# A perceiver block: two norms in a row as one, a bank for each chunk of the late tokens' input product, B and C of the first pair by products with rows of ones

## The chip, the core and the metric

The kernel runs on one core of a Trainium2 chip. The time is the device time of one execution in microseconds (us). Five engines work side by side: TensorE (PE in the profile; its weight loads are PEld), VectorE (DVE), ScalarE (ACT), GpSimd (POOL) and SyncE (SP), which here only issues DMAs. Each engine runs its own instructions in order and waits on semaphores for the others. Products of TensorE land in PSUM, which has 8 banks of 512 fp32 values per partition.

## The reference, cut to what matters

The input is x of 8 batches by 64 tokens by 512, so 512 tokens in all. Three blocks follow each other, each added to x.

```
x = x + cross_attention(layernorm(x), ctx)                 # 16 heads, 1601 context rows, masked
x = x + two_track_mamba(layernorm(x))                      # its own first step is a layernorm too
x = x + mixture_of_experts(layernorm(x))                   # 8 experts, 2 for each token

def layernorm(x):      m = mean(x); v = var(x); return (x - m) / sqrt(v + 1e-5)
def mamba(h):          # h: the normed tokens; d_inner 1024, n 16, r 64; two tracks with other weights
    x, z  = split(h @ in_w.T)
    x     = silu(causal depthwise conv of width 4 (x) + conv_b)
    x_dbl = x @ x_w.T                                      # 64 columns for dt, 16 for B, 16 for C
    dt    = softplus(x_dbl[:, :64] @ dtp_w.T + dtp_b)
    per step: h = exp(dt * A) * h + (dt * x) * B ;  y = sum over n of h * C
    return ((y + x * D) * silu(z)) @ mout_w.T
```

Two layernorms without weights stand between the first addition and the products of mamba: that of the block and mamba's own, whose weight and bias (`nw`, `nb`) are applied after it.

## The kernel before, in words

The context that the mask lets through is at most 400 rows here, and the kernel has a path for that case, which is the one that runs (`narrow`). A second path for the general case is in the program as well and does not run.

**Attention.** A loop over 8 batches, in each of which 4 pairs of heads are done while the next batch's K and V are projected. Every second batch a group of 128 tokens is complete, and `out_product(c)` multiplies it with the output weights (tile `ap`, L424), adds it to x (L425), and norms it twice (`layernorm_chunk`, lines L86 to L97: statistics on DVE, Ln and Exp on ACT for the reciprocal root, one Newton step on DVE, and the subtraction and scaling of 128x512). `normed(c, l1)` transposes the result on TensorE (`tpl`, L435) and writes it, with weight and bias, to `oT` (L437). The first three groups are done inside the loop. The fourth comes after it: its tokens are called the late tokens (`LATE = T - P`).

**Start of mamba.** For the first track the product with `in_w` and the convolution are done early for the first 384 tokens (`x_early`, beside the last batch). For the late 128 tokens they follow the last `normed`: `in_product` (L237) makes 8 chunks of 128 channels, four to a PSUM tile of one bank (`ipl`), so two tiles. `begin(c)` on ACT (L732) scales a chunk by the conv's last weight, `convolved` on DVE adds the other three weights (L257, three instructions for a chunk), ACT applies Silu to the whole chunk of 512 tokens (L742), and TensorE multiplies it with `x_w` into `xd` (`x_product`, L276). In `begin` and `convolved` the order is written out by hand with `keep`, which holds an instruction to the order of the program on its engine. Where it isn't used a scheduler chooses.

**From xd to the first scan.** ACT copies `xd` to `xdb` (96 rows: 64 for dt, 16 for B, 16 for C; L281). SP writes the B and C rows to HBM (`bcd`, L283) and reads them back, each row broadcast to all partitions, in 8 loads of 1 MB, one for each pair of state numbers n (`load_bc`, L793, tile `bc`). Meanwhile `dt_product` (L801), `dt_act`, `dt_log` and `dt_rest` make dt and du = dt * x of the first chunk. Then the loop over 8 chunks times 8 pairs runs: ACT makes `da` in PSUM (exp, L1032), POOL makes `db` = du * B (L1036), DVE scans (`hs`, L996) and multiplies by C (`hc`, L1005), TensorE sums the pairs up (`yp`, L1015). Column 0 of each batch in `da` is set to zero once (L784). Jobs that `beside` lists are done between the pairs: the other track's input product (`ix`), its convolution, the next chunk's dt.

**PSUM pools.** In the first part: `mm` 3 banks, `tp` 2, `sp` 2, `op` 1. In the second: `da0` and `da1` 2 each, `hs` 2, `mm` 1, `yp` 1.

Of the kernel before, what the change touches and what calls it, by code (L numbers as in the profile page):

```python
# [10 lines left out]
F32 = mybir.dt.float32  # L11
# [6 lines left out]
P = 128  # L18
B, S, D = 8, 64, 512
T = B * S  # L20
# [29 lines left out]
def perceiver_block(ctx: ExitStack, tc: tile.TileContext, a: dict, out: bass.AP):  # L50
# [11 lines left out]
    make_identity(nc, ident)  # L62
    eps = const.tile([P, 1], F32, name="eps")
    nc.gpsimd.memset(eps, EPS)
    one = const.tile([P, 1], F32, name="one")
    nc.gpsimd.memset(one, 1.0)
    mean_f = const.tile([P, P], F32, name="mean_f")
# [2 lines left out]
    def col(name, i, n=1):  # L70
        o = _COLS[name][0] + i
        return vec[:, o : o + n]
# [6 lines left out]
        nc.vector.reciprocal(rs, std)  # L79
        return rs  # L80

    def layernorm_chunk(dst, src):

        st = small.tile([P, 6], F32, tag="lcst", name="lcst")
        mv = small.tile([P, 2], F32, tag="lcmv", name="lcmv")
        nc.vector.bn_stats(st, src)  # L86
        nc.vector.bn_aggr(mv, st)
        rs = small.tile([P, 1], F32, tag="lcrs", name="lcrs")
        nc.scalar.activation(rs, mv[:, 1:2], AF.Ln, bias=eps)
        nc.scalar.activation(rs, rs, AF.Exp, scale=-0.5)  # L90
        var = small.tile([P, 1], F32, tag="lcva", name="lcva")
        nc.vector.tensor_scalar(var, mv[:, 1:2], eps, -0.5, ALU.add, ALU.mult)
        r2 = small.tile([P, 1], F32, tag="lcr2", name="lcr2")
        nc.vector.tensor_tensor(r2, rs, rs, ALU.mult)
        nc.vector.tensor_scalar(r2, r2, var, 1.5, ALU.mult, ALU.add)
        nc.vector.tensor_tensor(rs, rs, r2, ALU.mult)
        nc.vector.tensor_scalar(dst, src, mv[:, 0:1], rs, ALU.subtract, ALU.mult)  # L97
# [97 lines left out]
    def block(general):  # L195
# [4 lines left out]
        with ExitStack() as ctx:  # L200
# [34 lines left out]
            def in_product(ip, iw, u, o=0, n=T):  # L235
                for k in range(ND):
                    nc.tensor.matmul(  # L237
                        ip, iw[:, k, u * P : (u + 1) * P], oT[k][:, o : o + n], start=(k == 0), stop=(k == ND - 1)
                    )
# [47 lines left out]
            with tc.tile_pool(name="at1", bufs=1) as at1, tc.tile_pool(name="at2", bufs=2) as at2, tc.tile_pool(  # L287
# [129 lines left out]
                def out_product(c):  # L417

                    tok = slice(c * P, (c + 1) * P)
                    for k in range(ND):  # L420
                        nc.scalar.activation(oT[k][:, tok], oT[k][:, tok], AF.Identity, bias=col("bv", k))
                    ap_ = pa.tile([P, D], F32, tag="mm", bufs=3, name="ap")
                    for k in range(ND):
                        nc.tensor.matmul(ap_, oT[k][:, tok], wo[:, k, :], start=(k == 0), stop=(k == ND - 1))  # L424
                    nc.vector.tensor_tensor(xr[:, c, :], xr[:, c, :], ap_, ALU.add)  # L425
                    l1 = vtile("l1")
                    layernorm_chunk(l1, xr[:, c, :])
                    layernorm_chunk(l1, l1)
                    return l1

                def normed(c, l1):
# [288 lines left out]


                xd = pa.tile([P, 2, 512], F32, tag="sp", bufs=1, name="xd0")[:, 0, :]
                ips = []
                for q in range(2):
                    ip = pa.tile([P, 4, P], F32, tag="mm", bufs=3, name="ipl")
                    for i in range(4):
                        in_product(ip[:, i, :], iws[q * 2 + i // 2], i % 2, LATE, P)
                        ips.append(ip[:, i, :])

                def begin(c):  # L730
                    w = c * DCONV + DCONV - 1
                    keep(nc.scalar.activation(  # L732
                        xs[0][c][:, LATE:], ips[c], AF.Identity, scale=col("cw0", w), bias=col("cb0", c)
                    ))

                for c in range(2):
                    begin(c)
                for c in range(NCH):
                    convolved(0, c, ips[c], LATE, P, begun=True)
                    if c + 2 < NCH:  # L740
                        begin(c + 2)
                    keep(nc.scalar.activation(xs[0][c], xs[0][c], AF.Silu))  # L742
                    x_product(xd, 0, c)
                x_done(0, xd)
# [20 lines left out]
            with tc.tile_pool(name="mb1", bufs=1) as mb1, tc.tile_pool(name="mb2", bufs=2) as mb2, tc.tile_pool(  # L765
# [14 lines left out]
                def by_batch(v):  # L780
                    return v.rearrange("p (b s) -> p b s", s=S)

                for da in das:
                    nc.vector.memset(da.rearrange("p n (b s) -> p (n b) s", s=S)[:, :, 0:1], 0.0)  # L784

                def bank(name):
                    return pm.tile([P, T], F32, tag="mm", name=name)

                def load_bc(t, n):

                    bcd, tiles = bcs[t]
                    tiles[n] = mb1.tile([P, 2, 2, T], F32, tag="bc", bufs=NS // 2 + 1, name=f"bc{t}_{n}")
                    nc.sync.dma_start(  # L793
                        tiles[n].rearrange("p o n t -> p o (n t)"),
                        bcd[:, n : n + 2, :].rearrange("o n t -> o (n t)").partition_broadcast(P),
                    )
# [36 lines left out]

                for n in range(0, NS, 2):
                    load_bc(0, n)
                e, r = dt_act(0, 0, dt_product(0, 0))
                for step in dt_rest(nc.vector, 0, 0, e, r, dt_log(e)):
                    pass
                ahead = {(0, 0): step}

                comb_all = mb1.tile([P, ND, T], F32, name="comb")
                comb = [comb_all[:, m, :] for m in range(ND)]
# [712 lines left out]
```

## Time and profile before

| what | value |
|---|---|
| median of 3 runs | 1346.03 us (1344.24 to 1346.55) |
| the profiled execution's own time | 1351.73 us |
| its span, first to last instruction | 1350.1 us |
| mean granted TensorE clock | 0.972 |
| busy: PE, DVE, ACT, POOL | 1197.1, 827.0, 572.4, 512.5 us |
| last group's `ap` added to x (L425) starts | 381.03 us |
| first late product (L237) starts | 388.91 us |
| `xdb` copy (L281) starts | 408.95 us |
| first scan (L996) starts | 421.72 us |

How to read it: all times within an execution are counted from the span's start. In answers of the trace a row has start, length, engine, line, operation, output and inputs, how many were merged, and in square brackets how long the engine was idle before it and what ended that. The chain of waits is followed back from the last instruction: at each step it names what released it. The windows give the busy time of each engine in a stretch of time, the granted clock of TensorE as a share of its full clock, the share of the DMA engines that were busy, and GB/s. Line numbers are those of the kernel before.

### The profile page before, as it was taken

Reading aid. Unit: us, or ns where it says so; the run is one execution under the profiler, and the core shown is the slowest. Engines: PE = TensorE matmul, PEld = TensorE weight load, DVE = VectorE, ACT = ScalarE, POOL = GpSimd, SP = SyncE. Lnnn points to the kernel's source line nnn. Section 1 sums busy time; section 2 is a strip of 40 time slices with the busy share of each in tenths; the row PEclk is TensorE's granted clock in tenths of the full one; section 3 lists DMA queues with packets and bytes.
Section 4 is the critical chain, followed back from the end, with each engine's and each line's share of the span. In section 5 each row is a group of like instructions: output and inputs, shape, how many; then the busy total and the mean of one; then the engine's idle time right before and its main releaser. Section 6 shows DMA issues by size and latency. Waiting matters only on the chain.

```text
span 1350.1 us, 14093 instructions
## 1 busy us (share of the span) xinstructions
PE 1197.1 (89%) x5030; PEld 718.1 (53%) x5030; DVE 827.0 (61%) x1226; ACT 572.4 (42%) x1152; POOL 512.5 (38%) x384
## 2 busy tenths in 40 slices
PE   4999999999976889889889988879799999999992
PEld 2444454444542333333333333324699999999981
DVE  5144443545756999999999999994423433443332
ACT  1133333333234566665655555550134523453440
POOL 4200000000024788888888888850210221022130
PEclk9999999999978999999999999999699999999996
DMA  6329900000027000100701010110891673476432
GB/s 226 132 67 300 298 3 1 0 1 0 1 79 262 16 31 1 31 16 23 267 17 31 16 47 17 54 31 2 318 348 61 238 285 120 167 285 260 167 118 68
DMA packets 95051, 148.71 MB, mean 110 GB/s; under 512 B 5968, under 2 KB 63584, under 8 KB 90864
## 3 DMA queue, kind: packets, MB, share of 16 engines
q1 hardware_dynamic: 89856, 131.31, 29.0%
q0 software_dynamic: 5104, 16.30, 3.4%
q8 instruction: 44, 0.72, 0.2%
q14 instruction: 47, 0.39, 0.1%
HBM read 122.95 MB, written 24.64 MB: 109 GB/s over the span
## 4 chain that ended last, share of the span: by engine, by line
PE 59%; DVE 28%; ACT 7%; DMA 2%; issue 2%; another core or an unknown queue 0%; POOL 0%; DVEq 0%; SPq 0%; POOLq 0%; ACTq 0%
DVE hs L996 17%; PE yp L1406 10%; PE hp L1361 9%; PE kp L393 7%; PE vp L551 6%; DVE hc L1005 6%; ACT da L1032 4%; PE yp L1015 3%; PE op L603 3%; PE sp L565 2%; PE atp L590 2%; PE ipe L237 2%; PE atp L591 2%; PE ap L424 1%; PE ip L852 1%
## 5 line engine op out<-in xcount | busy, mean ns | idle before, releaser
L1036 POOL TENSOR_TENSOR db<-du,bc 128x1024 f32<-128x1024 f32 x128 | 301.7, 2358 | 103.3 <-DVE hs L996 81.8
L996 DVE TENSOR_TENSOR_SCAN hs<-da,db 128x1024 f32<-128x1024 f32 x128 | 293.9, 2296 | 20.3 <-POOL db L1036 5.6
L1015 PE MATMUL yp<-hc,ident 128*128 128x512 f32 x512 | 248.1, 608 | 57.8 <-DVE hc L1005 57.0
L1032 ACT ACTIVATE da<-dt,an 128x504 f32<-128x504 f32 x256 | 174.9, 683 | 172.0 <-DVE hs L996 166.1
L1015 PEld LDWEIGHTS yp<-hc,ident 128*128 128x128 f32 x512 | 91.9, 190 | 202.6 <-DVE hc L1005 118.7
L1005 DVE TENSOR_TENSOR hc<-hs,bc 128x1024 f32<-128x1024 f32 x128 | 156.7, 1224 | 11.2 <-DVE hs L996 0.9
L1361 PE MATMUL hp<-xgT,w 128*128 128x192 f32 (+1 forms) x1024 | 155.0, 311 | 3.5 <-DVE xgT L1333 3.0
L1406 PE MATMUL yp<-h,w 128*128 128x192 f32 (+1 forms) x1024 | 151.8, 310 | 4.4 <-ACT h L1391 4.4
L1361 PEld LDWEIGHTS hp<-xgT,w 128*128 128x128 f32 x1024 | 150.5, 193 | 5.3 <-DVE xgT L1333 3.7
L1406 PEld LDWEIGHTS yp<-h,w 128*128 128x128 f32 x1024 | 149.2, 193 | 5.3 <-ACT h L1391 4.8
L393 PE MATMUL kp<-ctx,wk 128*128 128x400 f32 x256 | 93.6, 511 | 0.0
L383 POOL COPY qbd<-qT 32x256 f32<-32x256 f32 x32 | 12.6, 394 | 208.9 <-PE sp L565 207.6
L551 PE MATMUL vp<-wv,ctx 128*128 128x512 f32 x192 | 88.2, 604 | 0.0
L1368 ACT ACTIVATE h<-hp,ev 128x192 f32<-128x192 f32 (+1 forms) x128 | 50.8, 398 | 82.2 <-PE hp L1361 82.0
L1324 POOL DMA_DIRECT2D xg<-x_rows x11 | 6.0, 544 | 185.5 <-PE xtp L1330 175.8
L614 DVE COPY oT<-op 32x64 f32<-32x64 f32 x64 | 13.7, 215 | 93.6 <-PE op L603 93.2
L393 PEld LDWEIGHTS kp<-ctx,wk 128*128 128x128 f32 x256 | 46.4, 190 | 44.1 <-issue 14.1
L1423 DVE BATCH_NORM_STATS2 bs<-ytp 128x6 f32<-128x512 f32 (+1 forms) x13 | 8.5, 688 | 98.2 <-PE ytp L1421 98.2
L852 PE MATMUL ip<-oT,iw 128*128 128x512 f32 x128 | 60.6, 597 | 4.4 <-ACT x L910 3.3
L571 DVE CUSTOM_DVE_ANT_0 sc<-sp,madd,rsc 128x400 f32<-128x400 f32 x64 | 38.1, 629 | 38.7 <-PE sp L565 38.6
L1391 ACT ACTIVATE h<-h,ev 128x192 f32<-128x192 f32 (+1 forms) x128 | 55.9, 518 | 5.5 <-DVE h L1388 5.2
L1343 DVE TENSOR_TENSOR s<-h 128x768 f32<-128x768 f32 (+1 forms) x16 | 13.7, 857 | 72.1 <-ACT h L1368 72.1
(282 smaller groups left out, 1590.2 us busy)
## 6 DMA issues: line engine op xcount, KB each, us to landing
w<-in_w_dram SPq DMA_DIRECT2D x64, 1024.0 KB, 14.9
bc<-bcd SPq DMA_DIRECT2D x16, 1024.0 KB, 9.9
x_rows<-z SPq DMA_DIRECT2D x8, 1152.0 KB, 12.2
y_rows<-z SPq DMA_DIRECT2D x8, 1152.0 KB, 12.1
ctx<-in_ctx_dram SPq DMA_DIRECT2D x32, 200.0 KB, 4.0
iw<-in_fast_in_w_dram SPq DMA_DIRECT2D x8, 512.0 KB, 3.9
iw<-in_slow_in_w_dram SPq DMA_DIRECT2D x8, 512.0 KB, 3.5
mo<-in_slow_mout_w_dram SPq DMA_DIRECT2D x8, 512.0 KB, 4.0
```

The costliest lines, as they stand in the source:

```text
L393: nc.tensor.matmul(kp[:, :n], wk[:, k, ec * P : (ec + 1) * P], ctx_t[k][:, o : o + n], start=(k == 0), stop=(k == ND - 1),)
L551: nc.tensor.matmul(vp, ctxs[b][k][:, j * P : (j + 1) * P], wv[:, k, :], start=(k == 0), stop=(k == ND - 1))
L852: keep(nc.tensor.matmul(s[key], w[:, k, u * P : (u + 1) * P], oT[k], start=(k == 0), stop=(k == ND - 1)))
L996: keep(nc.vector.tensor_tensor_scan(hs.rearrange("p n s -> p (n s)"), q["da"].rearrange("p n s -> p (n s)"), q["db"].rearrange("p n s -> p ...
L1005: keep(nc.vector.tensor_tensor(q["hc"], hs, bcs[t][1][n][:, 1], ALU.mult))
L1015: keep(nc.tensor.matmul(yp[0], ident, q["hc"][:, j, :], start=False, stop=(n + j == NS - 1)))
L1032: keep(nc.scalar.activation(by_batch(da[:, j, :])[:, :, 1:], by_batch(dt)[:, :, 1:], AF.Exp, scale=an[:, t, k : k + 1]))
L1036: keep(nc.gpsimd.tensor_tensor(db, du.rearrange("p (o s) -> p o s", o=1).to_broadcast([P, 2, T]), bc[:, 0], ALU.mult))
L1361: nc.tensor.matmul(hp, st["w1"][k][:, i * P : (i + 1) * P], st["xgT"][:, k, :n], start=(k == 0), stop=(k == ND - 1),)
L1368: nc.scalar.activation(h[:, i, :], hp, AF.Relu, bias=st["ev"][:, i : i + 1])
L1391: nc.scalar.activation(h[:, i, :], h[:, i, :], AF.Identity, bias=st["ev"][:, NF + f : NF + f + 1], scale=st["ev"][:, f : f + 1],)
L1406: nc.tensor.matmul(yp, ws[i // 4][:, i % 4, m * P : (m + 1) * P], st["h"][:, i, :], start=(i == 0), stop=(i == NF - 1),)
```

## The change

Three edits that lie close to each other in time.

1. `layernorm_chunk` gets an argument `twice`. The norm of a norm is worked out in one: with variance v, the second one's root is that of v(1 + eps) + eps^2 instead of v + eps. `out_product` calls it once instead of twice. A constant `eps2` is made at the start.
2. Each late chunk gets a PSUM bank of its own, in turn from `mm` and `tp`. Four products are issued ahead, the others one for each chunk. `begin` runs one chunk ahead of `convolved` instead of two.
3. B and C of the first pair (n = 0 and 1, first track) don't come through HBM. A matrix `picks` on POOL has ones in one row and zeros elsewhere; its product with `xdb` puts that row of `xdb` on all partitions. Four such products go to PSUM (`da1` for B, a tile of `hs` for C), DVE copies B and ACT copies C into the `bc` tile. The load of that tile is left out. The zeroing of `da` moves behind the first `dt_rest` in the text.

```diff
+    eps2 = const.tile([P, 1], F32, name="eps2")
+    nc.gpsimd.memset(eps2, EPS * EPS)
...
-        nc.scalar.activation(rs, mv[:, 1:2], AF.Ln, bias=eps)
+        nc.scalar.activation(rs, mv[:, 1:2], AF.Ln, bias=eps2 if twice else eps, scale=1.0 + EPS if twice else 1.0)
         nc.scalar.activation(rs, rs, AF.Exp, scale=-0.5)
...
-            nc.vector.tensor_scalar(var, mv[:, 1:2], eps, -0.5, ALU.add, ALU.mult)
+        if twice:
+            nc.vector.tensor_scalar(var, mv[:, 1:2], -0.5 * (1.0 + EPS), -0.5 * EPS * EPS, ALU.mult, ALU.add)
+        else:
+            nc.vector.tensor_scalar(var, mv[:, 1:2], eps, -0.5, ALU.add, ALU.mult)
...
-                    layernorm_chunk(l1, xr[:, c, :])
-                    layernorm_chunk(l1, l1)
+                    layernorm_chunk(l1, xr[:, c, :], twice=True)
...
-                ips = []
-                for q in range(2):
-                    ip = pa.tile([P, 4, P], F32, tag="mm", bufs=3, name="ipl")
-                    for i in range(4):
-                        in_product(ip[:, i, :], iws[q * 2 + i // 2], i % 2, LATE, P)
-                        ips.append(ip[:, i, :])
+                ips = {}
+
+                def late_product(c):
+                    if c < NCH:
+                        ips[c] = pa.tile([P, P], F32, tag=("mm", "tp")[c % 2], bufs=(3, 2)[c % 2], name="ipl")
+                        in_product(ips[c], iws[c // 2], c % 2, LATE, P)
...
-                for c in range(2):
-                    begin(c)
+                for c in range(4):
+                    late_product(c)
+                begin(0)
                 for c in range(NCH):
+                    begin(c + 1)
                     convolved(0, c, ips[c], LATE, P, begun=True)
-                    if c + 2 < NCH:
-                        begin(c + 2)
+                    late_product(c + 4)
                     keep(nc.scalar.activation(xs[0][c], xs[0][c], AF.Silu))
                     x_product(xd, 0, c)
...
-                for da in das:
-                    nc.vector.memset(da.rearrange("p n (b s) -> p (n b) s", s=S)[:, :, 0:1], 0.0)
...
+                    if (t, n) == (0, 0):
+
+                        return
...
-                e, r = dt_act(0, 0, dt_product(0, 0))
-                for step in dt_rest(nc.vector, 0, 0, e, r, dt_log(e)):
+                picks = mb1.tile([P, 4, P], F32, tag="xp", name="picks")
+                rows = slice(0, R + 2 * NS)
+                for o in range(2):
+                    for j in range(2):
+                        i = R + o * NS + j
+                        nc.gpsimd.tensor_scalar(picks[rows, o * 2 + j, :], ones[rows, :], ident[rows, i : i + 1], None, ALU.mult)
+                dp = dt_product(0, 0)
+
+                hs = pm.tile([P, 2, T], F32, tag="hs", name="c0")
+                for o, dst in enumerate((das[1], hs)):
+                    for j in range(2):
+                        keep(nc.tensor.matmul(dst[:, j, :], picks[rows, o * 2 + j, :], xdbs[0], start=True, stop=True))
+                bc0 = bcs[0][1][0]
+                keep(nc.vector.tensor_copy(bc0[:, 0], das[1]))
+                e, r = dt_act(0, 0, dp)
+                lu = dt_log(e)
+                keep(nc.scalar.copy(bc0[:, 1], hs))
+                for step in dt_rest(nc.vector, 0, 0, e, r, lu):
                     pass
                 ahead = {(0, 0): step}
+                for da in das:
+                    nc.vector.memset(da.rearrange("p n (b s) -> p (n b) s", s=S)[:, :, 0:1], 0.0)
```

## The prediction

> **What bounds the kernel now.** I read the page's busy shares and chain first, then the chain of waits from 340 to 450 us, the timeline there, and windows of 2 us.
>
> ```profile
> PE 1197.1 (89%) x5030; PEld 718.1 (53%) x5030; DVE 827.0 (61%) x1226; ACT 572.4 (42%) x1152; POOL 512.5 (38%) x384
> PE 59%; DVE 28%; ACT 7%; DMA 2%; issue 2%; another core or an unknown queue 0%; POOL 0%; DVEq 0%; SPq 0%; POOLq 0%; ACTq 0%
> ```
>
> As a whole the kernel is TensorE's, but none of the three edits takes a product off the path. They lie between the end of attention and the first scan, where TensorE is mostly idle. What ends last there is told by the chain of waits:
>
> ```profile
> 384.48 0.70 DVE lcst L86
> ...
> 386.62 0.56 DVE l L97
> ...
> 387.31 1.10 PE tpl L435 x4
> ...
> 388.91 5.74 PE ipl L237 x32
> ...
> 394.67 0.81 ACT x L732 x2
> ...
> 408.95 0.59 ACT xdb L281
> 409.56 2.98 DMA bcd<-xdb
> 412.56 6.65 DMA bc<-bcd
> ...
> 419.34 2.35 POOL db L1036
> ...
> 421.72 2.31 DVE hs L996
> ```
>
> The reader is to see four things: the second norm is on the path (it begins with `lcst` at 384.48); begin(0) waits for 32 product records, a whole bank of four chunks; after `xdb` the path goes through HBM and back; and then to the first scan. From there DVE leads (`hs` 2.30, `hc` 1.23, one pair each 3.69 us), so an earlier first scan moves everything behind it. The timeline shows why the convolution is slow:
>
> ```profile
> 395.51 1.11 DVE L257 SCALAR_TENSOR_TENSOR x<-ipl,vec,x 128x126 f32<-128x126 f32 x3 [5.70 <-ACT x L732]
> 396.65 0.46 ACT L732 ACTIVATE x<-ipl,vec 128x128 f32<-128x128 f32 x1 [1.18 <-DVE x L257]
> 397.13 1.28 ACT L742 ACT_TABLE_LOAD   x1
> 397.14 1.11 DVE L257 SCALAR_TENSOR_TENSOR x<-ipl,vec,x 128x126 f32<-128x126 f32 x3 [0.53 <-ACT x L732]
> ```
>
> begin(2) waits for conv 0 and conv 1 waits for begin(2), though neither uses the other's data. They read the same bank, and the program keeps two engines out of one bank. Last, the clock:
>
> ```profile
> 378.00:380.00 2.00, 0.94 (x2) 0.36 (x2) 0.06 (x1) 0.81 (x3) 0.00 (x0) 0.81 0.00 0
> 390.00:392.00 2.00, 2.00 (x11) 2.00 (x11) 0.00 (x0) 0.00 (x0) 1.79 (x6) 0.50 0.51 124
> 392.00:394.00 2.00, 2.00 (x16) 2.00 (x15) 0.00 (x0) 0.00 (x0) 0.06 (x1) 0.78 0.41 111
> 404.00:406.00 2.00, 1.47 (x4) 0.30 (x3) 1.37 (x6) 0.97 (x2) 0.00 (x0) 1.00 0.00 0
> ```
>
> The granted clock (third number from the end) falls to 0.50 at about 379.2 and is full again from about 392.9: the first late products run at half clock, 0.20 us apart, later 0.11.
>
> **Part 1, the norm.** In the last group the second norm runs from 384.48 to 387.18; with the step to it 2.73 us (387.18 less 384.45, the end of the first `l`). All of it is on the path: minus 2.73. The one that stays has the same instructions; its changed `lcva` (0.21) runs beside Ln and Exp on ACT (0.29 and 0.20), as now. The first three groups give nothing: from 149 to 167 us TensorE goes from product to product, the norm's result is there at 164.2 and `tpl` starts at 166.66 in its turn. Were that cover gone they would be worth up to 2.7 each. `eps2` is one POOL memset (0.12), hidden: the start hangs on the load of x until 12.02.
>
> **Part 2, the banks.** I count from the first late product, T (388.91 now). In the built order of the changed kernel chunks 0 and 1 are interleaved first: 16 records at 0.203 at half clock, the last landing at T+3.5, instead of 32 landing at T+5.73. begin(0) takes 0.46, conv 0 starts at T+4.0 (now T+6.60) and ends at T+5.1. Here the change has a wait of its own: the Silu table load (1.28) now stands right behind begin(1) and waits for conv 0; begin(2) is queued behind it. So: load to T+6.4, Silu 0 until begin(2) may start 0.54 later, begin(2) 0.46, conv 2 at T+7.45 (now 399.43, T+10.52). From there ACT needs 0.54 + 0.46 + 0.03 = 1.03 from the end of conv c to the end of begin(c+2), and conv c+1 lasts 1.11, so DVE runs through: 6 chunks by 1.11 end conv 7 at T+14.1. Now it ends at 407.04, T+18.1. What follows (Silu 7, `x_product`, `xdb`) is as long as now: minus 4.0, I take 4.1 with the event waits between them.
>
> TensorE must keep up: 64 product records and 16 of `x_product`. Products of chunks 5 to 7 stand between `x_product` 0 and 3 on its queue and wait for banks that conv 0, 1 and 3 free. At full clock a chunk costs 0.9 + 0.9 of TensorE against conv's 1.11, for three chunks only, and begin(5) is due at T+10.2 while its product is done by T+8.7. That is cover of about 1.5 us; without it the loss is worked out below as a rival. The weight loads that SP issues when these products free the old ones move by less than 2 us; they are wanted after 419 us.
>
> Here a rule speaks against the change. The Trainium skill, "TensorE: Matmul & The Clock Gate", section "A second HAM failure mode: psum-queue depth-cycling", says that a kernel cycling through PSUM banks makes TensorE idle so often between groups that its clock swings between half and full. By it the late products would stay at 0.50, and part 2 would cost 7.4 us (rival D). The nearest row is 404 to 406 us: TensorE busy 1.47 of 2 us in pieces, each ended by a wait for Silu, clock 1.00. That row decides for me; the changed stage is busier than it. The same page ("What's actually happening") lets the clock fall after an idle window of some 3.4 us; the idle stretch before `tpl` shrinks from 6.3 to 3.6 us. If the clock stayed full, the first two chunks would take 16 times 0.11 and 1.5 us more would be won. But the row of 378 to 380 shows the fall before that stretch, with TensorE still at work, so I keep half clock.
>
> **Part 3, B and C.** I count from the end of `xdb`, X (409.54 now). Now `bc` lands at X+9.67, `db` starts at X+9.80 and the first scan at X+12.18. du ends at X+6.58 and is not what is waited for. In the changed kernel TensorE does `dp` (2 records) and then B (4) and C (4), 0.46 apart (four `yp` records take 1.98), the last needing 0.6: B is there at X+3.05 with two semaphore waits of 0.05, C at X+4.9. No row shows a DVE copy of 128x1024 from PSUM; the copy of 128x384 (L594) takes 0.55 and `hc`, as wide and out of PSUM, 1.224; between 1.2 and 1.5 (2.67 times 0.55) I take `hc`'s: the copy ends at X+4.3. `dt_rest` is queued behind it on DVE: its first step starts now at X+3.18, then at X+4.33, 1.15 late, and du ends at X+7.75. ACT's copy of C (1.1 to 1.3, by 0.68 for 504) is between Ln (ends X+3.85) and `dgd`, ends by X+6.2, and dt is due at X+7.0: hidden, with 0.8 to spare. `db` runs X+7.8 to X+10.1, first scan X+10.15: minus 2.0. Were the B copy free it would be minus 3.2; at 2.5 us, minus 0.8.
>
> `picks` are four POOL instructions of 96x128. No row has that shape: memsets of 128x128 take 0.21, a tensor_scalar of 128x512 on POOL 1.94. By either end, 0.8 or 7.8 for the four, they are hidden: POOL waits 3.35 for `pb` there, its four adds (4.94) end at 400.35 now, and `e` needs them only at X+1.3; `picks` are read after X. The nearer row says 2. The two memsets of `da` (0.05 each) are on DVE ahead of the second step. SP issues one load less, so pair 1 gets the place of pair 0 in the queue and lands at X+9.67; its scan is due at X+13.85, needs `db` (2.35) started by X+11.4, so 1.7 us to spare. What is late next is DVE itself. The ACT work of the next chunk (`e`, `r`, then `ix` on TensorE) starts 1.15 later after X; the product `ix` is then done at about X+19.6 and its convolution stands on DVE at X+21.0.
>
> **Sum.** 2.73 + 4.1 + 2.0 = 8.8 us. Against the profiled execution (1351.73; span 1350.1 and 1.6 around it) that is 1342.9; it is 5.7 above the median of the runs, so against the median, 1337.2. Behind the first scan the instruction order of every engine is the old one, so nothing there gives it back.
>
> **The rivals.** B: TensorE's supply fails a little. The clock turns full one window later (3.4 us) and begin(5) to begin(7) wait for their products, up to 2.5 us: 1339.8. For it: it was at half clock for 4.0 us of late products. Against it: cover of 1.5. C: pair 1 comes late. If its load needs the median of all `bc` loads, 9.9 us from issue instead of 6.65, it lands at X+12.9 and the second scan slips by 1.5, and if DVE's copy takes 1.5 another 0.3 is lost: 1339.0. Against it: the first load of a batch has always the least ahead of it. D ends on the other side: TensorE stays at half clock all through the late chunks, because its products are now in pieces with waits between. Then 64 records at 0.203 and 16 at 0.85 make 26.6 us of TensorE plus 1.5 at the ends, X at T+28 instead of T+20.6: plus 7.4; B at X+5.3 brings the first scan to X+12.4, plus 0.2; with the norm's minus 2.73 the sum is plus 4.9: 1350.9. It decides from the point where some 60% of that work runs at half clock: X must come 23.2 after T for no gain, so 21.7 of TensorE, between 14.4 (all at full clock) and 26.6. Against it stands the row of 404 to 406. E: the change doesn't do what it says: the first scan is earlier, but the loop behind it hangs on work of ACT or TensorE that is not; then 2 to 8 are given back: at the end 1346. Against it: the chain of waits goes from the first scan to 453 us over DVE alone.
>
> **How the numbers follow.** The sum as it stands has 0.76, B 0.09, C 0.08, E 0.04, D 0.03. The sum's own bounds are 1334.0 (clock full early 1.5, B copy cheaper, spread of the runs 1.2) to 1340; B and C reach 1341.5. About 0.2% (2.7 us) is what a measurement of this kernel can tell from no change. Faster by more than that: 0.94; same 0.03; slower 0.03.
>
> **What would show it.** From L425 to `tpl` 3.5 us instead of 6.3. From the first late product to conv 0 about 4.0, and no idle of DVE before L257 between chunks 2 and 7. From the first late product to the end of `xdb` 16.5 (20.6). First `db` with DVE, not DMA, as what ended its wait; first scan 10.15 after `xdb` (12.18). Wrong: the clock at 0.50 behind T+7, a DMA ahead of the second `db` that pushes the second scan, or TensorE ahead of `begin`.

## The result: 12.4 us faster in the first comparison, 10 to 11 in three more

The changed kernel takes 1333.53 us (median, 1331.85 to 1334.06) and the kernel before, beside it, 1345.73. The ratio is 0.9908 [0.9893, 0.9923], which is 12.4 us less, 10.4 to 14.4. The forecast was 1337.2 us, or 8.8 less, in a range from 1334.0 to 1341.5: the sign was right, the gain was larger than the range allowed for. Measured three more times, on three chips, the gain was 10.0 (7.7 to 12.1), 10.2 (8.5 to 12.1) and 11.3 us (9.4 to 13.2).

The page of the changed kernel first, its busy shares and its chain by engine:

```profile
PE 1197.1 (90%) x5038; PEld 719.7 (54%) x5038; DVE 820.8 (62%) x1199; ACT 571.7 (43%) x1145; POOL 514.8 (39%) x389
PE 58%; DVE 29%; ACT 7%; DMA 2%; issue 2%; POOL 1%; DVEq 0%; SPq 0%; POOLq 0%; ACTq 0%
```

TensorE's busy time is the old one to 0.1 us, though 8 records were added; DVE has 6.2 us less to do, of which most lay where it cost nothing. The chain of the changed kernel, from the last group's addition to `xdb` (start, length, what):

```profile
378.69 0.70 DVE xr L431
...
381.55 0.56 DVE l L103
...
382.25 1.10 PE tpl L440 x4
...
383.83 7.12 PE ipl L243 x48
390.96 1.00 PE xd L282 x2
...
394.56 0.89 PE ipl L243 x8
395.45 4.31 PE xd L282 x10
...
399.78 0.59 ACT xdb L287
```

Three things are to be seen. One norm stands where two stood: 3.56 us from the addition to `tpl`, as against 6.28. From the first late product to `xdb` it is 15.95 us and not 20.0. And what the chain consists of has changed: in the kernel before it changed between TensorE, ACT and DVE, now it is TensorE from 383.83 to 399.76 without a gap. The timeline of the same stretch:

```profile
387.69 2.13 DVE L263 SCALAR_TENSOR_TENSOR x<-ipl,vec,x 128x126 f32<-128x126 f32 x6 [2.96 <-ACT x L738]
...
388.88 1.28 ACT L749 ACT_TABLE_LOAD   x1 [0.87 <-DVE x L263]
...
391.19 6.56 DVE L263 SCALAR_TENSOR_TENSOR x<-ipl,vec,x 128x126 f32<-128x126 f32 x18 [1.37 <-ACT x L738]
...
403.49 1.23 DVE L856 COPY bc<-da 128x1024 f32<-128x1024 f32 x1 [2.98 <-PE da L854]
...
408.10 2.35 POOL L1061 TENSOR_TENSOR db<-du,bc 128x1024 f32<-128x1024 f32 x1 [12.52 <-DVE du L837]
410.49 2.30 DVE L1021 TENSOR_TENSOR_SCAN hs<-da,db 128x1024 f32<-128x1024 f32 x1 [2.47 <-POOL db L1061]
410.98 2.35 POOL L1061 TENSOR_TENSOR db<-du,bc 128x1024 f32<-128x1024 f32 x1 [0.53 <-DMA bc<-bcd]
```

Conv 0 starts at 387.69, conv 2 at 391.19, and six convolutions follow each other without a gap. The first `db` waits for `du` and no longer for a load; the second waits 0.53 for its load, which harms nothing, since its scan comes after the first scan and its `hc`. The windows of 2 us (the number behind POOL's is the granted clock):

```profile
384.00:386.00 2.00, 2.00 (x10) 2.00 (x11) 0.74 (x3) 0.00 (x0) 1.92 (x5) 0.50 0.53 136
388.00:390.00 2.00, 2.00 (x20) 2.00 (x19) 1.68 (x6) 1.13 (x2) 1.39 (x3) 1.00 0.59 156
```

TensorE is busy all the time in both, with 10 records at half clock and 20 at full.

### The profile page after: what moved, and what is told of

Read it like the earlier page. It is cut to its first block, busy times and chain, and to the rows that moved or that the text cites. A ratio compares the mean times of both kernels' runs of the same rounds, so it can differ in the third digit from the quotient of the medians.

```text
span 1330.2 us, 14074 instructions
## 1 busy us (share of the span) xinstructions
PE 1197.1 (90%) x5038; PEld 719.7 (54%) x5038; DVE 820.8 (62%) x1199; ACT 571.7 (43%) x1145; POOL 514.8 (39%) x389
## 4 chain that ended last, share of the span: by engine, by line
PE 58%; DVE 29%; ACT 7%; DMA 2%; issue 2%; POOL 1%; DVEq 0%; SPq 0%; POOLq 0%; ACTq 0%
DVE hs L1021 18%; PE yp L1431 10%; PE hp L1386 9%; PE kp L399 7%; PE vp L556 7%; DVE hc L1030 6%; ACT da L1057 5%; PE op L608 3%; PE sp L570 2%; PE yp L1040 2%; PE atp L595 2%; PE ipe L243 2%; PE atp L596 2%; PE ap L430 1%; PE qp L370 1%
## 5 line engine op out<-in xcount | busy, mean ns | idle before, releaser
L1021 DVE TENSOR_TENSOR_SCAN hs<-da,db 128x1024 f32<-128x1024 f32 x128 | 293.9, 2296 | 17.2 <-POOL db L1061 2.5
L399 PEld LDWEIGHTS kp<-ctx,wk 128*128 128x128 f32 x256 | 46.3, 189 | 44.2 <-issue 14.1
L877 PE MATMUL ip<-oT,iw 128*128 128x512 f32 x128 | 63.7, 623 | 4.4 <-ACT x L935 3.3
L556 PEld LDWEIGHTS vp<-wv,ctx 128*128 128x128 f32 x192 | 34.7, 189 | 40.1 <-issue 39.2
## 6 DMA issues: line engine op xcount, KB each, us to landing
bc<-bcd SPq DMA_DIRECT2D x15, 1024.0 KB, 10.8
x_rows<-z SPq DMA_DIRECT2D x8, 1152.0 KB, 12.1
y_rows<-z SPq DMA_DIRECT2D x8, 1152.0 KB, 12.1
```

What stands on the lines that cost most here:

```text
L399: nc.tensor.matmul(kp[:, :n], wk[:, k, ec * P : (ec + 1) * P], ctx_t[k][:, o : o + n], start=(k == 0), stop=(k == ND - 1),)
L556: nc.tensor.matmul(vp, ctxs[b][k][:, j * P : (j + 1) * P], wv[:, k, :], start=(k == 0), stop=(k == ND - 1))
L877: keep(nc.tensor.matmul(s[key], w[:, k, u * P : (u + 1) * P], oT[k], start=(k == 0), stop=(k == ND - 1)))
L1021: keep(nc.vector.tensor_tensor_scan(hs.rearrange("p n s -> p (n s)"), q["da"].rearrange("p n s -> p (n s)"), q["db"].rearrange("p n s -> p ...
```

## Where the microseconds are

All profiles are cut at the same places. "To `ap`" is from the start to the point where the last record of the last attention product begins; "stage", where all three edits lie, from there to the first scan; "loop" from there to the first product with `pw`; "router" to the experts' first second-layer product; then 283.7 or 283.8 us of experts in every profile, left out here; "end" from the last write of `y_rows` to the end. "Wait" is what DVE waits in the end for the eight gathers `yb`. Gain: one less the measured ratio, times the median of the kernel before on the same chip, with its interval where it was timed (by the plain medians e1's is 1.3 instead of 2.4). The stretches are differences of rounded starts, so good to 0.1.

| kernel | gain, us | to `ap` | stage | loop | router | end | wait |
|---|---|---|---|---|---|---|---|
| before | | 379.9 | 41.8 | 504.7 | 95.2 | 44.8 | 16.7 |
| b1_before_again | | 378.7 | 41.2 | 504.6 | 89.9 | 43.8 | 16.4 |
| b2_before_third | | 379.1 | 41.7 | 504.7 | 89.7 | 44.0 | 16.3 |
| changed, first time | 12.4 (10.4 to 14.4) | 378.1 | 32.4 | 504.6 | 89.5 | 41.9 | 14.9 |
| e4_all_again | 10.0 (7.7 to 12.1) | 379.8 | 32.9 | 504.7 | 92.5 | 42.0 | 14.9 |
| e5_all_third | 10.2 (8.5 to 12.1) | 380.1 | 32.5 | 504.7 | 94.6 | 41.2 | 14.4 |
| s3_all_fourth | 11.3 (9.4 to 13.2) | 380.0 | 32.9 | 504.7 | 89.5 | 42.0 | 15.0 |
| e1_norm_alone | 2.4 (0.5 to 4.3) | 377.1 | 40.6 | 503.4 | 94.3 | 41.3 | 14.8 |
| e2_banks_alone | 3.0 (1.5 to 4.4) | 379.0 | 37.9 | 505.2 | 94.7 | 45.1 | 17.1 |
| e3_bc_alone | 5.0 (3.0 to 7.0) | 380.2 | 39.6 | 503.4 | 93.2 | 43.4 | 16.2 |
| e6_begin_two_ahead | 10.4 (8.5 to 12.3) | 378.9 | 32.6 | 504.7 | 93.7 | 42.6 | 15.9 |
| e7_b_by_act | 10.6 (8.8 to 12.4) | 378.1 | 32.7 | 503.6 | 94.7 | 41.2 | 14.5 |
| e8_both | 11.5 (9.6 to 13.2) | 379.0 | 31.5 | 503.6 | 97.0 | 41.4 | 14.4 |
| e9_both_warm | 12.9 (10.5 to 15.2) | 379.6 | 29.5 | 503.5 | 90.6 | 43.9 | 15.9 |
| e10_all_warm | 11.8 (9.7 to 14.1) | 379.2 | 30.5 | 504.6 | 90.5 | 42.1 | 15.7 |
| e11_both_warm_behind | 13.2 (11.4 to 15.1) | 380.3 | 29.5 | 503.6 | 90.4 | 42.6 | 15.4 |
| s1_before_eps2 | 1.3 (0.1 to 2.6) | 378.8 | 41.6 | 504.7 | 89.5 | 43.3 | 15.7 |
| s5_before_eps2_again | | 378.6 | 41.4 | 504.7 | 90.4 | 43.4 | 17.4 |
| s2_all_no_eps2 | 10.1 (8.3 to 12.0) | 378.5 | 32.4 | 504.7 | 89.4 | 42.5 | 15.8 |
| s4_norm_no_eps2 | 3.9 (1.9 to 5.9) | 379.7 | 39.7 | 503.3 | 90.3 | 42.6 | 14.5 |

The first pair of profiles differs by 19.9 us in its span: 1.8 to `ap`, 9.4 in the stage, 0.1 in the loop, 5.7 in the router, 2.9 at the end. The router's 5.7 is, in the chain before, a wait for something that the trace doesn't name ("another core or an unknown queue", 5.70 us from 964.88). It isn't the change's, for the length of this stretch goes with the chip and not with the kernel: on the chip of e1 to e4 and on that of e5 to e8 it is 92.5 to 97.0, and on the three others (b1, b2, e9 and e10; s1 to s3 and e11; s4 and s5) 89.4 to 90.6, with and without each edit on either side. The kernel before is slower there too (medians of 1348.15 and 1347.79 us, against 1343.03 to 1344.24). The chip of the first pair is not on record. Why chips, or their hours, differ in it is not known. The stage, against the mean of the five profiles that have none of the three edits (41.5), is 32.4 to 32.9 in the five of the changed kernel and of it without `eps2`, mean 32.6: 8.9 us.

## The experiments

Theory A: the stage gives about the 8.8 us that were forecast, and what the first comparison has beyond it is chance outside the stage. Theory B: the change brings something of its own in another place. A rival of another kind for the stage: TensorE ends it, not the convolutions.

**Each edit alone**, with the other two as before. Edits: e1 `+ layernorm_chunk(l1, xr[:, c, :], twice=True)` with `eps2`; e2 the eight tiles `ipl` of one bank and the new order of `begin`; e3 `picks` and the copies of B and C, and the load of the first pair left out. e4 is the changed kernel, unaltered, beside them.

> The one norm alone, all else as before. Theory A (the parts are what the prediction counted, and the 3.4 us beyond its sum lie outside the changed stage): from the start of the addition to x of the last group to its tpl 3.55 us instead of 6.3; time 2.7 us under before, no more. Theory B (a part is worth more than counted; the first suspect is the norm, whose work the first three groups do beside TensorE's products and whose end decides how long TensorE idles before tpl): 5 to 6 us under before, and the extra shows ahead of the late products or as full clock in the first of them.

> A bank for each late chunk alone; both norms and all eight loads as before. Theory A: 4.1 us under before; from the first late product to conv 0 about 3.9 instead of 6.6, to the end of xdb 16.5 instead of 20.6. Theory B: more than 5.5 under before with the same 16.5, so that the rest must come from behind the first scan. Rival D of the prediction (the clock stays at half in the late chunks) would show 0.50 behind 7 us after the first late product and a time above before.

> B and C of the first pair by products alone; norms and banks as before. Theory A: 2.0 us under before; first scan 10.1 after the end of xdb instead of 12.2. Theory B: 4 or more under before, because one load of 1 MB less also lets the loads behind it start earlier. Rival C (the second pair comes late): the second scan waits, and the gain is below 1.

> The changed kernel once more, as the sum to compare the three parts with. Theory A: 9 to 12 us under before, the three parts adding up to 8.8 and the rest a matter of the runs (granted clock at the start and at the last group's output product, landing of the first load, transfers at the end). Theory B: 12 or more under before and the parts alone add up to as much.

Measured: 2.4, 3.0 and 5.0 us, in sum 10.4, and 10.0 together. Within intervals of some 2 us each the edits add up. From the profiles: the norm takes the step from the addition to `tpl` from 7.0 to 4.2 us (to the end of `tpl`), but in e1 the half clock lasted to 389.06, and late products took so long that conv 0 came 8.3 after the first one instead of 6.6; 1.7 of the 2.8 was lost again. The banks take the first late product to `xdb` from 20.1 to 16.3, B and C take `xdb` to the first scan from 12.7 to 10.7. These are the forecast's terms (2.73, 4.1, 2.0) to 0.3 us. e3's 5.0 is more than its 2.0. Of the rest, 1.3 is in its loop, which is shorter in four steps of some 0.35 between pairs. e1 and s4, the norm alone, have the same four steps. The changed kernel has them too, and loses each again eight pairs later, so its loop is as long as before: the parts and the whole agree in sum, but not place by place. Why some kernels keep these steps is not known.

**Two moves that should each give a microsecond**, on top of the change, and the change a third time. e6:

```diff
-                begin(0)
+                for c in range(2):
+                    begin(c)
                 for c in range(NCH):
-                    begin(c + 1)
                     convolved(0, c, ips[c], LATE, P, begun=True)
+                    begin(c + 2)
                     late_product(c + 4)
```

e7 (e8 is both):

```diff
-                keep(nc.vector.tensor_copy(bc0[:, 0], das[1]))
+                keep(nc.vector.memset(das[0]..., 0.0))
...
-                keep(nc.scalar.copy(bc0[:, 1], hs))
+                keep(nc.scalar.copy(bc0[:, 0], das[1]))
...
-                for da in das:
-                    nc.vector.memset(da..., 0.0)
+                keep(nc.vector.memset(das[1]..., 0.0))
+                keep(nc.vector.tensor_copy(bc0[:, 1], hs))
```

> The changed kernel, unaltered, measured a third time against the kernel before. Theory A (what the first comparison had beyond 8.9 us comes from stages that the change doesn't touch, and differs from run to run): 8.9 us less, ratio 0.9934, with an interval that may reach from 0.991 to 0.995; in its profile the three stages stay as they were (end of the chunk's add to the last tpl 4.2, first late product to the end of xdb 16.0, from there to the first scan 10.7, landmarks as in the table of the runs so far), while the MoE's stretch (308.2 in the first changed run, 311.1 in the second) and the tail differ again by some us. Theory B (the change brings 1.5 to 3 us more in a place of its own behind the first scan): the ratio is 0.992 or lower a third time, and one and the same later stretch is short by 1.5 us in each changed run.

> All three edits, but begin(0) and begin(1) ahead of the convolutions and begin(c+2) behind conv c, as the kernel before had it, each chunk still with its own bank; so begin(2) no longer stands behind the Silu table load. If what still holds conv 2 is the queue on ACT (table load behind conv 0, begin(2) behind it, as the prediction's part 2 says): conv 2 begins at 6.1 after the first late product instead of 7.36, conv 7 ends at 12.9 instead of 13.9, and the time is 1.0 us below the changed kernel's, if the last products keep up. If TensorE's supply at half clock holds it instead (begin(2) waits for its product, products of chunk 2 done at about 5.3 after the first): conv 2 moves by less than 0.5 and the time is the changed kernel's.

> All three edits, but B is copied out of its bank by ACT (1.0) and C by DVE (1.2) behind du, so that dt_rest on DVE no longer stands behind the copy of B. If the copy on DVE was on the path, as the prediction's part 3 costs it (1.15 late): du ends at 6.7 after xdb and the first scan begins at 9.0 instead of 10.1, 1.1 us below the changed kernel. If ACT's chain (copy of B ahead of or between e, r and Ln) takes its place: du moves by less than 0.3 and the time stays; with the copy of B late (db waits for ACT) the scan comes at 10 or later, and C's copy by DVE delays the first hc by up to 1.2.

> The two above together: first scan 2.1 us earlier than in the changed kernel, so 11.0 us under the kernel before (ratio 0.9918) by theory A; if only one of them gives its microsecond, 9.9 (0.9926); if both waits only move elsewhere, as the changed kernel (0.9934).

e6 gained nothing that can be told (0.5 us by the medians beside it, 1337.86 and 1338.36). Its chain says why:

```profile
384.69 7.34 PE ipl L243 x48
...
396.43 4.31 PE xd L282 x10
...
400.76 0.59 ACT xdb L287
```

And its timeline, the convolutions on DVE:

```profile
388.57 3.15 DVE L263 SCALAR_TENSOR_TENSOR x<-ipl,vec,x 128x126 f32<-128x126 f32 x9 [2.98 <-ACT x L738]
...
396.96 1.11 DVE L263 SCALAR_TENSOR_TENSOR x<-ipl,vec,x 128x126 f32<-128x126 f32 x3 [0.63 <-ACT x L738]
```

Conv 2 now follows conv 1 at once, and conv 7 ends 13.4 us after the first late product, 0.5 earlier than in the changed kernel. But TensorE is busy without a gap to 400.74, and `xdb` starts 16.07 after the first late product (384.69), where it was 15.95. In e7 the first scan is 9.7 after the start of `xdb` (10.7), as expected, and that microsecond was lost in the same stage: `xdb` came 17.2 after the first late product. e8, both moves, has `xdb` at 16.1 and the first scan 9.7 after it, so one of the two microseconds; its gain of 11.5 can't be told from the change's 10.2 beside it. e5, the change a third time, has the stage at 32.5 and an end of 41.2, again shorter than that of the kernel before. Here is the window of e7:

```profile
388.00:390.00 2.00, 2.00 (x11) 2.00 (x10) 1.75 (x6) 1.21 (x2) 1.41 (x3) 0.50 0.71 130
```

Half clock to 390.00, 11 records where the changed kernel had 20 in these 2 us. All late products and `x_product` at full clock take 14.4 us; half clock costs half of its length. In the changed kernel 3.2 us of it make 16.0, in e7 6.1 make 17.4 (measured 17.2), in e6 3.6 make 16.2 (16.1). So it seems that TensorE with its clock ends this stage, not the convolutions.

**The clock kept up by products that nobody reads.** e9 is e8, e10 the change as it is, both with 4 such products ahead of the last attention product and 12 behind it; e11 is e8 with the 12 alone, with operands that come last. Of e9 and e10, cut:

```diff
+                xds = pa.tile([P, 2, 512], F32, tag="sp", bufs=1, name="xd0")
...
+                            xds[:, 1, :P], oT[0][:, (NT - 1) * P :], wo[:, 0, :P], start=True, stop=True
```

> Both small moves (begin two ahead, B by ACT) on top of the change, and 16 products of 128x128 that nobody reads, 4 ahead of the last product of the attention's output and 12 behind it, so that TensorE is busy where it was idle for 3.6 us ahead of the transposes. In the changed kernel's runs TensorE goes from product to product without a gap from the first late product to xdb, and the time from one to the other follows the half-clock stretch in it (16.0 with 3.2 us at half clock, 17.2 with 6.1). If TensorE's supply and its clock end this stage, the granted clock stays 1.00 past the late products, first late product to xdb falls from 16.0 to 14.4 or to what the convolutions then need (about 14.9), and the time is 1.1 to 1.6 below that of both small moves alone. If the clock falls all the same, the 12 products take 5.3 us at half clock, the transposes start 1.7 later and the time is 1.7 higher. If the convolutions end the stage, as the prediction's part 2 says, nothing changes.

> The change as it is, with the same 16 products that nobody reads. If TensorE's supply ends the stage: first late product to xdb from 16.0 to 14.9 at most by the convolutions (begin(2) still stands behind the Silu table load), 1.1 below the changed kernel, ratio about 0.9917 to 0.992 against the kernel before. If the prediction's part 2 has it right (begin(2) behind the table load behind conv 0): conv 0 starts 1.5 earlier and the whole chain with it, 1.5 below the changed kernel. If the clock falls all the same: 1.7 above it.

> Both small moves and the 12 products that nobody reads behind the attention's last output product alone, with that product's own operands, so that none of them can come ahead of it (in the run with 16 of them, 6 records of 0.94 us ran ahead of waiting work and the output's last product ended 1.2 us later than in the other runs). If the 12 suffice to keep the clock: first late product to xdb 14.4, no 1.2 lost, so 1.2 below that run and about 14 under the kernel before (ratio 0.9896). If the clock falls since the 4 ahead are missing: products at half clock, transposes up to 1.7 later, ratio 0.993.

Windows of e10:

```profile
380.00:382.00 2.00, 2.00 (x21) 2.00 (x20) 1.56 (x4) 0.45 (x2) 0.00 (x0) 1.00 0.00 0
384.00:386.00 2.00, 1.50 (x14) 1.46 (x14) 1.37 (x4) 0.00 (x0) 1.31 (x2) 1.00 0.40 111
```

The clock stays at 1.00, and from the first late product to `xdb` it is 14.4 us in all three, which is TensorE's queue at full clock without a gap. e10 alone doesn't decide what ends the stage: it is 1.5 us shorter than in the change, and the convolutions begin 1.5 earlier too (2.36 instead of 3.86 after the first late product), as part 2 of the prediction would have had it. e10 beside e9 decides it. The last convolutions and `xdb` of e10:

```profile
390.39 6.56 DVE L263 SCALAR_TENSOR_TENSOR x<-ipl,vec,x 128x126 f32<-128x126 f32 x18 [1.37 <-ACT x L750]
...
398.98 0.59 ACT xdb L287
```

The same of e9:

```profile
395.56 1.11 DVE L263 SCALAR_TENSOR_TENSOR x<-ipl,vec,x 128x126 f32<-128x126 f32 x3 [0.64 <-ACT x L750]
...
399.36 0.59 ACT xdb L287
```

Counted from the first late product (384.54 and 384.92), conv 7 ends at 12.4 in e10 and at 11.8 in e9, and `xdb` starts at 14.4 in both. Convolutions that are 0.6 us earlier change nothing, so TensorE ends the stage.

In e9 and e10 the products ahead cost 1.2 us themselves ("to `ap`" less the first K product: 343.8 instead of 342.6); in e11 they don't. e11 has the lowest median of the study, 1331.56 beside 1333.46 for the change on the same chip, where the two gains' intervals still overlap; its gain of 13.2 is not told from e9's 12.9, and is less than the 14 that were expected. Of the 3.4 us of the stage and 1.1 of the loop that its profile has over the change's (s3), 1.8 are given back in the other places (0.3, 0.9 and 0.6), which differ that much between runs; 2.7 are left in the spans and 1.9 in the medians.

**What lies beyond the stage.** First, two more profiles of the kernel before, without an edit:

> The kernel before, unaltered, for a second profile of it. Theory A (the 1 to 3.5 us that the change gained beyond its own stages are run to run): the stretch from the first second-layer product of the experts to the end, 328.5 in the first profile and 325.0 to 325.7 in three profiles of the changed kernel, comes out below 327 in this run or the next. Theory B (it is systematic): above 328 in both.

> The kernel before, a third profile. The same two expectations: A, the stretch from the experts' first second-layer product to the end below 327 here or in the second profile; B, above 328 in both. From the first pp product to that second-layer product (95.2 in the first profile, 89.5 to 94.6 in the changed kernel's): A, it differs by over 1 us among the three profiles of before; B, within 0.5.

The stretch that was named came out at 327.5 and 327.8, between the two expectations, so it told nothing by itself. The router's did (89.9 and 89.7 after 95.2): theory A, and by the table above it goes with the chip. Cut at `y_rows`, the end did too: 43.8 and 44.0, near the 44.8 of the first profile, where the changed kernel has 41.2 to 42.0. That speaks for theory B, and the place is the eight gathers `yb`. One suspect was `eps2`, which moves every tile behind it by 32 bytes in SBUF, `yb` too. s1 and s5 add it alone, s2 and s4 take it away (s4 from the norm alone), s3 is the change beside them:

```diff
-    eps2 = const.tile([P, 1], F32, name="eps2")
-    nc.gpsimd.memset(eps2, EPS * EPS)
...
-        nc.scalar.activation(rs, mv[:, 1:2], AF.Ln, bias=eps2 if twice else eps, scale=1.0 + EPS if twice else 1.0)
+        nc.scalar.activation(rs, mv[:, 1:2], AF.Ln, bias=eps, scale=1.0 + EPS if twice else 1.0)
```

> The kernel before with nothing of the change but the tile eps2 (one number per partition) and its memset; nobody reads it. In the built program it moves every tile of SBUF behind it by 32 bytes, and yb, into which the eight last gathers write rows of 2 KB, from 32 past a multiple of 64 to a multiple of 64. In the profiles so far, from the first add of a gathered row to the last takes 12.8 to 13.7 us in the five kernels without eps2 and 11.0 to 12.6 in the nine with it. If the place in SBUF does it: that stretch is 11.0 to 12.6 here, and the time 1.0 to 2.0 us below the kernel before (ratio 0.9985 to 0.9993). If it comes with the norm's own change (fewer instructions, other data) or by chance: 12.8 to 13.7 and a ratio of 1.000.

> The whole change, but the bias of the one norm's Ln is the old eps tile instead of eps2 (its variance is off by one part in 100,000), so that eps2 is gone and every tile lies where it lay before. If the place in SBUF does it: from the first add of a gathered row to the last 12.8 to 13.7 instead of 11.0 to 12.6, and the time 1.0 to 2.0 us above the changed kernel, so that the rest of the change is left: 8.9 below the kernel before (ratio 0.9934). If not: as the changed kernel (0.9925), stretch 11.0 to 12.6.

> The changed kernel beside the two above on the same chip. Place in SBUF: stretch of the gathered rows 11.0 to 12.6, ratio 0.992 to 0.9927, and 1.0 to 2.0 us under the version without eps2. Otherwise: level with it.

> The norm's edit alone, without eps2 (bias of its Ln from the old eps tile, variance off by one part in 100,000): tiles lie where they lay before. What DVE waits for the eight gathers at the end was 16.2 to 17.1 us without any of it (five profiles), 15.7 with eps2 alone, 15.8 with everything but eps2, 14.8 to 15.0 with both. If the two act on their own, half each: 15.8 here, and 2.8 from the stage plus 0.9: 3.7 below the kernel before (ratio 0.9973). If eps2's place alone counts and the 15.8 was chance: 16.4 or more, 2.8 below (0.9979). If the norm's edit counts alone and eps2's 15.7 was chance: 15.0 or less, 4.5 below (0.9967).

> The kernel before with eps2 and nothing else, a second profile. If eps2's place acts on the gathers: DVE waits 15.4 to 16.0 for them again. If the 15.7 was chance: 16.2 to 17.1 as in the kernels without it.

The first group left it open: `eps2` alone gained 1.3 us, hardly told from nothing, and everything but `eps2` as much as the change within the intervals. From the start of the first add of a gathered row to the end of the last took 12.4 us in both, which speaks for the place in s1 and against it in s2, and the waits were 15.7 and 15.8, in the middle. The second decides by DVE's waits at the end (us in total, how often, the longest). Those of the norm without `eps2`, s4:

```profile
DVE xr L1454 <- DMA yb<-y_rows,slot: 14.5, 8, 9.4
```

And those of `eps2` without the norm, s5:

```profile
DVE xr L1453 <- DMA yb<-y_rows,slot: 17.4, 6, 9.4
```

So the place in SBUF isn't what decides. (s4's time doesn't tell: its interval of 1.9 to 5.9 holds all three expectations.) Over all profiles the wait is 15.7 to 17.4 (mean 16.5) in the seven without the norm's edit and 14.4 to 15.9 (15.1) in the thirteen with it, and the end 44.0 and 42.1 us in the mean: 1.9 us go with the norm's edit, with or without `eps2`, and with or without the other two. The chip has a share in this mean: four of the thirteen ran on a chip on which none without the edit was profiled. Chip by chip the end is shorter with the edit by 2.6 us (e1 and e4 against e2 and e3), by 0.9 (e9 and e10 against b1 and b2, where e10 has all of it and e9 none), by 0.9 (s2, s3 and e11 against s1) and by 0.8 (s4 against s5); in the first pair it is 2.9. So the sign is the same everywhere, and the size is known only as some 1 to 3 us. Why the last gathers land earlier when nine instructions per group are gone, the last of them some 900 us before, is not settled: the program is shorter, and the data differ in their last digits; neither was tried apart.

## Why the prediction was wrong, point by point

- **The norm** (2.73 forecast): 6.28 to 3.56 us, which is 2.72. Right. What was forecast at nothing for the first three groups is right for their stage: "to `ap`" less the first K product is 342.5 to 343.0 in all kernels without extra products.
- **The banks** (4.1): conv 0 at T+3.86 (forecast 4.0), conv 2 at T+7.36 (7.45), end of conv 7 at T+13.9 (14.1), `xdb` ends at T+16.54 (16.5 in the forecast's list). Every number right, one reason wrong, so that the sum came out right by luck. The step "TensorE must keep up ... cover of about 1.5" failed: after the edit TensorE has no gap from T to T+15.93, and it ends the stage, about 0.4 us behind what the convolutions alone would have needed (conv 7 ends at 397.75, its Silu runs from 397.84 to 398.47, and 0.86 for the last product makes 399.33; TensorE was done at 399.76). The two were so near each other that the sum hid it; e6 and e7 hinted at it, and e9 beside e10 settled it. The mistake in the step: it looked at three chunks where both kinds of product meet, with no half clock in them, and not at TensorE's whole queue. The forecast had what it takes: the 14.4 at full clock of its rival D and the half clock of the first products (1.5 to 2 us lost) make about 16, beside the 15.9 at which its convolutions let `xdb` start.
- **B and C** (2.0): `xdb` end to first scan 10.12 (forecast 10.15), B's copy by DVE 1.23 (1.22), du at X+7.65 (7.75), ACT's copy of C 1.01. Right. The second pair's load landed 10.6 after the end of `xdb` and not 9.67, inside the cover of 1.7.
- **The rule against the change**: the oscillating clock (rival D) did not come; the row that was weighed against it decided rightly. The swing between half and full that the Trainium skill ("TensorE: Matmul & The Clock Gate", section "A second HAM failure mode: psum-queue depth-cycling") tells of needs a TensorE that idles often, and with a bank for each chunk it doesn't idle at all here. The page tells of a swing; that the clock would stay at 0.50, and the 7.4 us, were the forecast's own bound.
- **The sum**: 8.8 forecast, 8.9 in the stage. The step that failed is the term for everything behind the first scan, which was put at nothing: "Behind the first scan the instruction order of every engine is the old one, so nothing there gives it back." It asked only whether something is lost there, and took the same order for the same time. The loop is indeed as long as before (504.6 to 504.8 us in either kernel). The end got shorter with the norm's edit, by 1.9 us in the mean and by 0.8 to 2.9 chip by chip. 8.9 and 1.9 make 10.8, which lies inside all four intervals of the change; 8.9 alone lies inside two of them. What makes the last gathers earlier stays open.
- **The range**: its lower end, 1334.0, is 12.0 below the 1346.03 it was counted from. It had 1.2 us for the spread of the runs and nothing for a gain outside the stage. The gain of one comparison of four runs is uncertain by 2.0, and the median gain of the four comparisons is 10.8; so both terms were too small. The three later gains (10.0, 10.2 and 11.3) are all smaller than 12.0, so that the first one passed it is in part chance: its 12.4 is 10.8 and 1.6 more, inside its interval.

## What to carry to other kernels

When a change lets an engine run through, add up the whole queue of the next engine over the stage, at the clock that it will have there, and take the later of the two; two sums within a microsecond of each other mean that the next improvement of either gives nothing. A short idle stretch of TensorE ahead of a burst can cost more in the burst than where it stands: 12 products that nobody reads in a gap of 3.6 us took 1.6 us off the time from the first late product to `xdb` (16.1 in e8, 14.4 in e11). And leave room in a range for stages that the change doesn't touch: here they gave 1 to 3 us that no step of the sum could name, and from chip to chip one stretch differed by up to 7 us.

## What the runs showed of the hardware

- In every profile the times at which the granted clock changes lie whole multiples of 3.413 us apart: in the changed kernel 380.18, 387.00, 407.48 and 414.31, which is 2, 6 and 2 of them. The grid lies at another offset from the program's start in each run (0.15 to 3.35 us). That agrees with the Trainium skill ("TensorE: Matmul & The Clock Gate", section "What's actually happening", free-running windows of 3413 ns). It has a price for comparing kernels. Up to `xdb` the changed kernel and e7 have the same instructions at nearly the same times, yet half clock cost the one 1.5 us (15.95 less 14.4) and the other 2.8 (17.2), with a grid 0.42 earlier in e7. The windows of the grid that end at full clock in the change and stay at half clock in e7:

```profile
383.59:387.00 3.41, 3.17 (x15) 3.17 (x16) 1.15 (x4) 0.00 (x0) 2.79 (x7) 0.50 0.40 87
```

```profile
383.17:386.59 3.42, 2.91 (x13) 2.72 (x13) 1.37 (x4) 0.00 (x0) 2.36 (x7) 0.50 0.40 87
```

- The same section lets the clock fall after an idle window of some 3.4 us. Here the measurement differs: it fell at 380.18 in the changed kernel, 1.5 us after TensorE's last product (378.66), at the end of a window in which TensorE was busy for 1.13 us. With products in the gap, which left 0.92 us of it idle (e10, below), it stayed at 1.00.

```profile
376.77:380.18 3.41, 1.13 (x2) 0.30 (x2) 1.43 (x3) 0.65 (x3) 0.00 (x0) 1.00 0.00 0
```

```profile
383.41 0.63 PE L442 MATMUL tpl<-ident,l 128*128 128x128 f32 x4 [0.92 <-DVE l L103]
```

- Copies of 128x1024 out of PSUM: 1.23 us on DVE, 1.01 on ACT. The four `picks` of 96x128 on POOL took 0.59 each, between the bounds of 0.2 and 1.94.
